# A graph network in two layers: edge maxima and the Wh sum moved forward on VectorE in even steps, divisions joined in odd steps, and a new order in the first five steps

## The chip, the cores and the metric

The kernel runs on one core of one Trainium2 chip. A core has a matrix engine (TensorE, PE in the profile; its weight loads, PEld, overlap the matmuls), VectorE (DVE), ScalarE (ACT), GpSimd (POOL) and SyncE (SP), each with a queue of its own that it works off in order. Data come from and go to DRAM through DMA, and here nearly all transfers are issued by SP. The metric is device time in microseconds; the number that counts is the median of the runs. One further execution was profiled, and its trace is what the text quotes.

## The reference

128 graphs of 128 nodes with 512 features each, and an integer adjacency matrix for each graph. Two layers, both with a residual and a layer norm:

```
# layer 0: attention with 8 heads of 64
q, k, v = x @ Wq + bq, x @ Wk + bk, x @ Wv + bv
attn    = softmax(where(adj > 0, q k^T / 8, -1e9))      # over the keys
x       = layernorm(x + relu(attn v @ Wo + bo))
# layer 1: graph attention with one head
Wh      = x @ W
e       = leaky(s_i + s_j),  s_i = Wh @ a1,  s_j = Wh @ a2   # leaky: slope 0.2
att     = softmax(where(adj > 0, e, -9e15), axis=1)     # over the senders
x       = layernorm(x + leaky(att @ Wh))
```

All is in fp32. Every product with a weight matrix is done by Strassen's scheme: seven products of half-size blocks in place of eight, with sums of blocks before and after.

## The kernel before, in words

The kernel is a software pipeline over graphs. Step t of the main loop (line 987) handles graph t in the first stage and older graphs in later ones. Graphs go in groups of four for Q, K and V (21 block products, `group_steps`), in pairs for the attention's output product with Wo (`LayerZero`) and for the product with W (`LayerOne`). `group()` takes the next block product of a group, `pair()` the next of a pair. An even step holds a pair's products with W, an odd step those with Wo. Everything stands in the order that the loop writes down; no scheduler moves it. So the text of the loop is the order in every engine's queue.

What one step contains, as far as the change touches it:

- Two softmaxes start in an even step, `first` for graph t and `sm` for t+1 (`Softmax`). `scores` are TensorE's matmuls into PSUM (tile lg). `add` adds the mask on VectorE (L534), `reduce` takes the negated row maxima (L543), `exp` is one ScalarE instruction for each head (L554), `reciprocals` two of VectorE (L564), `divide` one of ScalarE for each head (L568). `store` writes the weights to DRAM (pa_dram, L575), `fetch` reads them back in four pieces (paz, L581), `transpose` turns the 32x32 blocks on VectorE (L587), and `attend` is the product with v (p_oT, L600). `first` is divided in its even step, `sm` in the odd step after; both are attended at the end of the odd step.
- `Edge` is layer 1 for one graph, seven steps back. `sender` adds s_i to the mask on ScalarE (e, L798), `store_sender` and `fetch_sender` send it through DRAM, `turn_blocks` ends its transposition (L817), `add` adds s_j (L820), `maxima` is leaky and row maximum (L825, L827), `exp` L831, `divide` a reciprocal and a multiplication on VectorE (L835, L836), `product` is the matmul with Wh (p_h, L841). One step later the same object is called `fin`: `residual` (L851, L852), `stats`, `rstd` (GpSimd), `apply` (L665) and `store` (L865).
- Of the seven block products of a pair, p1, p6, p7 and p4 accumulate in one PSUM bank, p_y, one after the other. Between them ScalarE copies the bank out (pr_t, L459), and the next product may not start before that copy has read. `c11` is the first result block; for `LayerOne` it is VectorE's addition into wh (L772), whose last column is s_i, so `sender` needs it.
- For a group, the weight blocks of V are too large to stay and come through a ring of three tiles (wv_n, L408), loaded one by one.
- In steps divisible by four GpSimd forms the block sums of the next group's inputs (xS, L276 to L279).

The first steps fill the pipeline and have branches of their own (t below 3, t = 4), which also hold work that is done once, such as the sums w1_chores. From END on, a list written out by hand empties it.

Of the kernel before, what the change touches and what calls it, by code (L numbers as in the profile page):

```python
# [24 lines left out]
def kernel(  # L25
# [225 lines left out]
    def load_x(b):  # L251
        X[b] = spread(x[b])
# [734 lines left out]
    for t in range(-3, END):  # L987
        pair_steps = []
        if t % GROUP == 1 and on(t + 3):
            rest = group_steps  # L990
            group_steps, v_pieces, fetch_v = products((t + 3) // GROUP)
            group_steps = rest + group_steps
        if t % 2 == 1 and on(t - 3):
            pair_steps = zero[(t - 3) // 2] = LayerZero((t - 3) // 2)
            pair_steps = pair_steps.steps()
        if t % 2 == 0 and on(t - 6):
            pair_steps = LayerOne((t - 6) // 2).steps()

        def group(n=1):
            for _ in range(min(n, len(group_steps))):  # L1000
                group_steps.pop(0)()
            for _ in range(min((3 if t == -3 else 2 if t >= 0 else 1) * n, len(chores))):
                chores.pop(0)()

        def w1_chores(n):
            for op in [w1_sums.pop(0) for _ in range(n)]:
                op()

        def pair(n=1):
            for _ in range(min(n, len(pair_steps))):  # L1010
                pair_steps.pop(0)()

        if on(t + 2):
            load_mask(t + 2)
        if t == 0:
            load_blocks(Wo, columns(wo), nc.sync, spread_rows=False)
            late_chores = right_blocks(places(wo)) + load_bias()
            w1_loads, w1_sums, w1_blocks = load_w1()
        if t == 1:
            chores += late_chores  # L1020

        if t % 2 == 0:

            first, sm = none, none
            if on(t):
                first, sm = (Softmax(b, first_homes.get(b)) for b in (t, t + 1))
            first.scores()
            sm.scores()
        coming.turn_blocks()
        if t % 2 == 1 and on(t - 3):  # L1030
            zero[(t - 3) // 2].by()
            zero[(t - 3) // 2].bw()
        if later and t > 4:
            later.pop().go_back()
        if t % 2 == 1:
            sm.exp(6, 7)
        if t == 5:
            group(2)
        if t < 3 and t % 2 == 0:
            first.maxima()  # L1040
            sm.add(0)
            sm.add(1)
            group(2)
            if on(t - 2):
                load_residual(t - 2)
            if t == 0 and on(GROUP):
                sum_x(1)()
            first.exp(0, 1, 2, 3)
            group()
            first.reciprocals(0)  # L1050
            first.exp(4, 5, 6, 7)
            first.reciprocals(1)
            sm.reduce()
            first.divide(0, 1, 2, 3)
            if t == 2:
                held[1].transpose()
            group()
            first.divide(4, 5, 6, 7)
            mask_float(t + 2)
        elif t < 3:  # L1060
            group(2)
            if on(t - 2):
                load_residual(t - 2)
            group()
            sm.reciprocals(0)
            sm.reciprocals(1)
            if t == 1:
                group()
            sm.divide(0, 1, 2, 3)
            first.transpose()  # L1070
            group()
            sm.divide(4, 5, 6, 7)
            if t == 1:
                group()
            if on(t + 2):
                mask_float(t + 2)
        elif t == 4:

            layer = later.pop()
            first.maxima()  # L1080
            group()
            layer.apply(0)
            sm.add(0)
            sm.add(1)
            load_residual(2)
            if on(8):
                sum_x(2)()
            first.exp(0, 1)
            group()
            first.exp(2, 3, 4, 5)  # L1090
            sm.reduce()
            group()
            layer.store(1)
            layer.store(0)
            layer.fetch(1)
            layer.fetch(0)
            w1_chores(3)
            first.exp(6, 7)
            group()
            first.reciprocals(0)  # L1100
            first.reciprocals(1)
            first.divide(0, 1, 2, 3, 4, 5, 6, 7)
            mask_float(6)
        else:
            if t % 2 == 0:
                first.maxima()
            group()
            if t % 2 == 0:
                sm.add(0)
                sm.add(1)  # L1110
            if t == 3:
                w1_chores(3)
            if t == 5:
                turn_x1(4)
                x1_sums()
            edge = coming
            edge.add()
            fin.residual()
            if on(t - 2):
                load_residual(t - 2)  # L1120
            if t % 2 == 1:
                sm.reciprocals(0)
                sm.reciprocals(1)
            edge.maxima()
            fin.stats()
            fin.rstd()
            x1_sums()
            if t % GROUP == 0 and on(t + GROUP):
                sum_x(t // GROUP + 1)()
            if t % 2 == 0:  # L1130
                pair()
                first.exp(0, 1, 2, 3)
                edge.exp()
                pair()
                first.exp(4, 5)
                sm.reduce()
                group()
                first.reciprocals(0)
                pair()
                first.exp(6)  # L1140
                fin.apply()
                fin.store()
                first.exp(7)
                edge.divide()
                pair()
                first.reciprocals(1)
                first.divide(0, 1, 2, 3)
            else:
                pair()
                sm.divide(0, 1)  # L1150
                edge.exp()
                sm.divide(2)
                pair()
                sm.divide(3, 4, 5)
                first.transpose()
                group()
                pair()
                fin.apply()
                fin.store()
                sm.divide(6, 7)  # L1160
                sm.store()
                edge.divide()
                pair()
            coming = Edge(t - 6) if on(t - 6) and t + 1 < END else none
            coming.sender()
            coming.store_sender()
            if t in (3, 5):
                w1_chores(2 if t == 3 else 4)
            if t == 5:
                for op in w1_blocks:  # L1170
                    op()
            group()
            if t % 2 == 0:
                first.divide(4, 5)
            pair()
            if t % 2 == 0:
                first.divide(6, 7)
            if on(t + 2):
                mask_float(t + 2)
            group()  # L1180
        if t % 2 == 0:
            first.store()
        elif t < 3:
            sm.store()
        if 0 <= t < 3:
            for load in w1_loads[4 * t : 4 * t + 4]:
                load()
        if t % 2 == 1:
            sm.fetch()
        if t >= 6:  # L1190
            coming.fetch_sender()
        if t % 2 == 0:
            first.fetch()
        for b in x_turns(t):
            transpose_x(b)
        for b in x_turns(t + 1):
            load_x(b)
        if on(t + 2):
            mask(t + 2)
        if t % 2 == 0:  # L1200
            sm.exp(0, 1, 2)
        pair()
        if t % 2 == 1 and t != 1:
            sm.transpose()
        pair()
        if t % 2 == 0:
            sm.exp(3, 4, 5)
        if t % 2 == 0 and on(t - 6):
            turn_x1(t)
        if t not in (0, 4):  # L1210
            group(21 if t % GROUP == 0 else 1)
        fin = edge
        fin.product()
        fin.copy()
        if t == 1:
            held = first, sm
        elif t == 2 or t % 2 == 1:

            both = held if t == 2 else (first, sm)
            for softmax in both:  # L1220
                softmax.attend()
            for softmax in both:
                softmax.copy()
            both[1].sum(0, 1, 2, 3)
# [183 lines left out]
```

## Time and profile before

| what | value |
|---|---|
| median of 3 runs | 2463.04 us (2461.87 to 2465.6) |
| profiled execution, own time | 2459.1 us |
| span of the profile | 2457.2 us |
| mean granted TensorE clock | 0.997 |
| DMA, mean | 161 GB/s, 395 MB |

A line of the groups and waits names the engine, the source line and the tile it writes. "PE p_y L448 <- ACT pr_t L459: total, times, longest" tells for how long in all, how often and at most how long TensorE stood before a matmul of line 448 for ScalarE's line 459. A row of the timeline has the start, the time, the engine, the line and the operation, the tiles written and read, and, in brackets, the idle time before it with what ended it. A row of the table by stage has the stretch, its length, and for PE, PEld, DVE, ACT and POOL the busy time with the number of instructions, then the granted clock, the share of the DMA engines and GB/s. SPq is SP's queue; the time of its rows is that of issuing.

### The profile page before, as it was taken

Reading aid. Unit: us, or ns where it says so; the run is one execution under the profiler, and the core shown is the slowest. Engines: PE = TensorE matmul, PEld = TensorE weight load, DVE = VectorE, ACT = ScalarE, POOL = GpSimd, SP = SyncE. Lnnn points to the kernel's source line nnn. Section 1 sums busy time; section 2 is a strip of 40 time slices with the busy share of each in tenths; the row PEclk is TensorE's granted clock in tenths of the full one; section 3 lists DMA queues with packets and bytes.
Section 4 is the critical chain, followed back from the end, with each engine's and each line's share of the span. In section 5 each row is a group of like instructions: output and inputs, shape, how many; then the busy total and the mean of one; then the engine's idle time right before and its main releaser. Section 6 shows DMA issues by size and latency. Waiting matters only on the chain.

```text
span 2457.2 us, 44158 instructions
## 1 busy us (share of the span) xinstructions
PE 2355.6 (96%) x13362; PEld 1972.3 (80%) x13362; DVE 1836.2 (75%) x3718; ACT 1517.7 (62%) x5459; POOL 770.5 (31%) x1191
## 2 busy tenths in 40 slices
PE   8999999999999999999999999999999999999997
PEld 7788888888888888888888788878888888888775
DVE  5677777777777777777777777777777777777768
ACT  3656656666656566566565565665666656656675
POOL 1232332323333323333233332333332332323326
PEclk9999999999999999999999999999999999999999
DMA  7555555555555555555555555545554555545443
GB/s 203 163 157 158 164 161 171 158 155 170 160 154 165 159 162 162 165 166 156 158 160 164 161 163 154 169 153 164 167 159 151 170 165 162 163 154 169 145 159 115
DMA packets 435565, 395.31 MB, mean 161 GB/s; under 512 B 108280, under 2 KB 339328, under 8 KB 435328
## 3 DMA queue, kind: packets, MB, share of 16 engines
q1 hardware_dynamic: 435008, 392.23, 51.6%
q8 instruction: 107, 1.75, 0.3%
q14 instruction: 130, 1.06, 0.1%
q10 hardware_dynamic: 320, 0.26, 0.0%
HBM read 248.58 MB, written 143.72 MB: 160 GB/s over the span
## 4 chain that ended last, share of the span: by engine, by line
PE 45%; DVE 25%; DMA 11%; ACT 9%; SPq 4%; issue 4%; POOL 1%; DVEq 0%; POOLq 0%; ACTq 0%
PE st_y L367 14%; PE p_y L448 9%; PE st_w L367 7%; DMA pa_dram<-pa 5%; PE p_w L448 5%; DVE pa L534 4%; ACT pa L568 4%; PE st_x L367 3%; PE p_h L841 3%; SPq L581 3%; DMA ez<-e_dram 3%; DMA paz<-pa_dram 2%; DVE pa L587 2%; DVE nmax L543 2%; DVE z L665 2%
## 5 line engine op out<-in xcount | busy, mean ns | idle before, releaser
L650 POOL TENSOR_SCALAR ve<-mv 128x1 f32<-128x1 f32 x256 | 70.3, 275 | 1529.3 <-DVE mv L646 1521.9
L554 ACT ACTIVATE pa<-pa,nmax 128x128 f32<-128x128 f32 x1008 | 394.6, 397 | 9.8 <-DVE nmax L543 9.5
L568 ACT ACTIVATE pa<-pa,rs 128x128 f32<-128x128 f32 x1008 | 334.1, 396 | 33.9 <-DVE rs L564 33.9
L587 DVE STREAM_TRANSPOSE pa<-paz 128x1024 f32<-128x1024 f32 x126 | 156.9, 1245 | 89.0 <-DMA ez<-e_dram 58.3
L459 ACT COPY pr_t<-p_y 128x257 f32<-128x257 f32 (+1 forms) x375 | 138.1, 368 | 126.5 <-PE p_y L448 125.7
L348 ACT ACTIVATE st_t<-st_y,b_cols 128x256 f32<-128x256 f32 x192 | 80.1, 468 | 190.9 <-PE st_y L367 190.8
L554 ACT ACTIVATION_READ_ACCUMULATOR pa<-pa,nmax 128x1 f32 x1008 | 195.1, 194 | 0.0
L344 ACT COPY st_t<-st_y 128x512 f32<-128x512 f32 x192 | 111.0, 578 | 135.5 <-issue 78.9
L600 PEld LDWEIGHTS p_oT<-pa,v 128*64 128x64 f32 x2016 | 108.0, 136 | 89.0 <-DVE pa L587 41.7
L614 ACT ACTIVATE oT<-p_oT,b_cols 128x128 f32<-128x128 f32 x504 | 141.2, 375 | 59.7 <-PE p_oT L600 59.4
L448 PE MATMUL p_y<-w,x1T 128*128 128x257 f32 x496 | 134.3, 393 | 37.2 <-ACT pr_t L459 35.6
L600 PE MATMUL p_oT<-pa,v 128*64 128x128 f32 x2016 | 132.6, 278 | 33.5 <-DVE pa L587 32.9
L534 DVE TENSOR_TENSOR pa<-lg,mf 128x512 f32<-128x512 f32 x252 | 160.9, 679 | 0.2 <-PE lg L520 0.2
L543 DVE TENSOR_REDUCE nmax<-pa 128x8 f32<-128x1024 f32 x126 | 151.7, 1204 | 2.3
L652 POOL TENSOR_TENSOR rstd<-ve,mhalf 128x1 f32<-128x1 f32 x256 | 146.5, 572 | 21.3
L448 PEld LDWEIGHTS p_y<-w,x1T 128*128 128x128 f32 x496 | 89.4, 190 | 70.8 <-ACT pr_t L459 58.5
L448 PE MATMUL p_y<-wo,oT 128*128 128x256 f32 x504 | 130.5, 382 | 4.0 <-ACT p_y L469 4.0
L520 PE MATMUL lg<-kT,qT 64*128 64x128 f32 x2048 | 132.1, 279 | 0.0
L448 PE MATMUL p_y<-w,x1S 128*128 128x257 f32 x496 | 129.9, 384 | 0.4 <-ACT wk L459 0.2
L448 PE MATMUL p_y<-wo,oS 128*128 128x256 f32 x504 | 129.5, 379 | 0.6 <-ACT pr_t L459 0.5
L520 PEld LDWEIGHTS lg<-kT,qT 64*128 64x128 f32 x2048 | 119.4, 188 | 12.3 <-issue 11.9
L367 PE MATMUL st_y<-wv_n,xT 128*128 128x256 f32 x512 | 122.4, 382 | 2.6 <-ACT st_t L344 2.6
(201 smaller groups left out, 5902.6 us busy)
## 6 DMA issues: line engine op xcount, KB each, us to landing
pa_dram<-pa SPq DMA_DIRECT2D x126, 512.0 KB, 2.9
paz<-pa_dram SPq DMA_DIRECT2D x504, 128.0 KB, 2.8
wv_n<-wv SPq DMA_DIRECT2D x224, 256.0 KB, 2.9
x<-in_x_dram SPq DMA_DIRECT2D x128, 256.0 KB, 2.9
x_dram<-x SPq DMA_DIRECT2D x128, 256.0 KB, 2.1
xz<-x_dram SPq DMA_DIRECT2D x512, 64.0 KB, 2.0
xz<-in_x_dram SPq DMA_DIRECT2D x496, 64.0 KB, 2.1
out_dram<-z SPq DMA_DIRECT2D x120, 256.0 KB, 2.1
```

Source lines behind the costliest of these rows:

```text
L367: nc.tensor.matmul(p[:, m, :], lhs, rhs, start=start and m == 0 and kc == 0, stop=True, skip_group_check=True,)
L448: nc.tensor.matmul(p[:, :width], xs()[n][:, kc, :], w[:, PLACE[n], kc, :], start=start and kc == 0, stop=True, skip_group_check=True,)
L459: nc.scalar.copy(t[:, :width], p[:, :width])
L520: nc.tensor.matmul(self.lg[r][:, c, :], q[rows, c, cols], k[rows, c, cols], start=c == 0, stop=True, skip_group_check=True,)
L534: nc.vector.tensor_add(by_head[:, r * NC : (r + 1) * NC], self.lg[r].rearrange("p c (b k) -> p c b k", b=4), mf.unsqueeze(1).to_broadcast( ...
L543: nc.vector.tensor_reduce(self.nmax, by_head, AX.XY, ALU.max, negate=True)
L554: nc.scalar.activation(self.pa[:, :, h, :], self.pa[:, :, h, :], AF.Exp, bias=self.nmax[:, h : h + 1], accum_out=self.sums[:, h : h + 1],)
L568: nc.scalar.activation(self.pa[:, :, h, :], self.pa[:, :, h, :], AF.Copy, scale=self.rs[:, h : h + 1])
L587: nc.vector.transpose(self.paT.rearrange("p h (a i) -> p a h i", i=32), self.paz.rearrange("p a (h k) -> p a h k", k=32),)
L600: nc.tensor.matmul(self.oT[r * HD : (r + 1) * HD, c, :], v[:, h * HD : (h + 1) * HD], self.paT[:, r * NC + c, :], start=c == 0, stop=True, ...
L614: nc.scalar.activation(OT[pair][:, c, h * P : (h + 1) * P], self.oT[:, c, :], AF.Identity, bias=b_cols[:, 1, c : c + 1],)
L652: nc.gpsimd.tensor_tensor(self.r, ve, mhalf, ALU.pow)
```

## The change

The steps of the loop are reordered; no instruction is added or taken away.

- Even steps from 6 on: `edge.maxima` goes ahead of `sm.add` and `fin.residual`. The pair product with `c11` goes ahead of `edge.divide`, and `fin.apply` and `fin.store` go behind both and behind the second reciprocals. Heads 6 and 7 of `first` get their exponentials together.
- Odd steps from 3 on: heads 3 to 7 of `sm` are divided in one go and `sm.store` follows directly, ahead of `first.transpose` and of `fin.store`.
- First steps: at t = 0 a further group product stands between the exponentials of `first`, and `sm`'s exponentials of heads 3 to 7 are all in t = 1. At t = 4 the w1 sums go to the end of the branch and one load of x comes forward.

```diff
-        if t % 2 == 1:
+        if t % 2 == 1 and t != 1:
             sm.exp(6, 7)
...
             first.reciprocals(0)
-            first.exp(4, 5, 6, 7)
+            first.exp(4, 5)
+            if t == 0:
+                group()
+            first.exp(6, 7)
             first.reciprocals(1)
...
                 load_residual(t - 2)
+            sm.exp(3, 4, 5, 6, 7)
             group()
...
-            w1_chores(3)
+            for b in x_turns(5)[:1]:
+                load_x(b)
             first.exp(6, 7)
...
             mask_float(6)
+            w1_chores(3)
         else:
             if t % 2 == 0:
                 first.maxima()
             group()
-            if t % 2 == 0:
-                sm.add(0)
-                sm.add(1)
...
             edge.add()
-            fin.residual()
+            if t % 2 == 0:
+                edge.maxima()
+                sm.add(0)
+                sm.add(1)
+                fin.residual()
+            else:
+                fin.residual()
+                sm.reciprocals(0)
+                sm.reciprocals(1)
+                edge.maxima()
             if on(t - 2):
                 load_residual(t - 2)
-            if t % 2 == 1:
-                sm.reciprocals(0)
-                sm.reciprocals(1)
-            edge.maxima()
             fin.stats()
...
                 pair()
-                first.exp(6)
+                first.exp(6, 7)
+                pair()
+                edge.divide()
+                first.reciprocals(1)
                 fin.apply()
                 fin.store()
-                first.exp(7)
-                edge.divide()
-                pair()
-                first.reciprocals(1)
                 first.divide(0, 1, 2, 3)
...
-                sm.divide(3, 4, 5)
+                sm.divide(3, 4, 5, 6, 7)
+                sm.store()
                 first.transpose()
                 group()
                 pair()
                 fin.apply()
                 fin.store()
-                sm.divide(6, 7)
-                sm.store()
                 edge.divide()
                 pair()
...
-        for b in x_turns(t + 1):
+        for b in x_turns(t + 1)[t == 4 :]:
             load_x(b)
...
-        if t % 2 == 0:
+        if t % 2 == 0 and t != 0:
             sm.exp(3, 4, 5)
```

## The prediction

> **What bounds the kernel now.** I read the busy shares first, then who TensorE waits for, then the timeline of one cycle of four steps.
>
> ```profile
> PE 2355.6 (96%) x13362; PEld 1972.3 (80%) x13362; DVE 1836.2 (75%) x3718; ACT 1517.7 (62%) x5459; POOL 770.5 (31%) x1191
> ```
>
> TensorE is busy for all but 101.6 us of 2457.2, so a change of order can win at most about 100 us here. The list of TensorE's waits, from 240 to 2340 us:
>
> ```profile
> PE p_y L448 <- ACT pr_t L459: 34.5, 41, 1.2
> PE p_oT L600 <- DVE pa L587: 28.7, 31, 1.7
> ```
>
> Two waits are all there is in the loop. Where they sit shows in the table by stage, one row for each step (a multiple of 4, then t = 1, 2, 3 modulo 4 in other cycles):
>
> ```profile
> 1067.80:1092.50 24.70, 21.87 (x143) 18.10 (x142) 18.41 (x33) 15.54 (x58) 10.13 (x13) 1.00 0.50 154
> 1016.80:1032.40 15.60, 15.60 (x72) 13.34 (x72) 10.75 (x24) 8.06 (x27) 3.70 (x6) 1.00 0.59 177
> 1032.40:1052.30 19.90, 19.90 (x136) 16.71 (x135) 17.02 (x34) 15.11 (x59) 5.49 (x10) 1.00 0.47 155
> 1052.30:1067.80 15.50, 15.50 (x71) 13.28 (x70) 10.89 (x25) 8.26 (x26) 4.20 (x8) 1.00 0.52 163
> ```
>
> Odd steps run without a gap; the stretch around a step divisible by 4 has 2.8 us of idle TensorE. First wait, in the even step (timeline, us from the start):
>
> ```profile
> 1081.09 0.40 ACT L831 ACTIVATE att<-att,nmax 128x128 f32<-128x128 f32 x1 [1.40 <-DVE nmax L827]
> 1082.98 1.38 DVE L665 TENSOR_SCALAR z<-z,mv,rstd 128x512 f32<-128x512 f32 x1
> 1084.47 1.11 DVE L836 TENSOR_SCALAR att<-att,rt 128x128 f32<-128x128 f32 x1
> 1085.50 0.42 DVE L772 TENSOR_TENSOR wh<-p_x,pr_t 128x257 f32<-128x257 f32 x1
> 1085.95 0.40 ACT L798 ACTIVATE e<-mf,wh 128x128 f32<-128x128 bf16 x1 [0.90 <-DVE wh L772]
> 1086.84 0.35 ACT L459 COPY pr_t<-p_y 128x257 f32<-128x257 f32 x1
> 1087.24 1.14 PE L448 MATMUL p_y<-w,x1T 128*128 128x257 f32 x4 [1.17 <-ACT pr_t L459]
> ```
>
> The fourth product into p_y must wait for ScalarE's copy of that bank (pr_t). ScalarE is late because it stood 1.40 us for the edge maximum and 0.90 us for the sum for Wh; that sum stood on VectorE behind fin.apply and the edge division. Second wait, at the end of the odd step before:
>
> ```profile
> 1060.14 0.70 ACT L568 ACTIVATE pa<-pa,rs 128x128 f32<-128x128 f32 x2
> 1061.30 0.34 SPq L865 DMA_DIRECT2D out_dram<-z  x1
> 1061.74 0.38 SPq L575 DMA_DIRECT2D pa_dram<-pa  x1
> 1064.61 3.16 SPq L581 DMA_DIRECT2D paz<-pa_dram  x4
> 1070.22 1.25 DVE L587 STREAM_TRANSPOSE pa<-paz 128x1024 f32<-128x1024 f32 x1 [2.99 <-DMA ez<-e_dram]
> 1071.52 1.09 PE L600 MATMUL p_oT<-pa,v 128*64 128x128 f32 x16 [1.66 <-DVE pa L587]
> ```
>
> The odd softmax's weights go out to DRAM and come back (L575, L581) before VectorE turns them; the way out began only at 1061.74, behind the output store. (The wait is put down to ez; the transpose reads paz, so it is the four paz loads.)
>
> [...] pa's store stood 0.9 us behind a z store that waited for VectorE. [...] L665 takes 504 ns at least and 1387 at most, L836 285 and 1116; the long ones lie where GpSimd's sums for the next group run (t divisible by 4). L772, one of whose operands is in PSUM, stays at 0.42 us. [...] the mean clock is 0.66 in 51 to 56 us and 0.57 in 82 to 86 us.
>
> **The change, part by part.** No arithmetic is added or removed; it moves work.
>
> *(a) Even steps, edge maxima ahead (L825, L827).* They end at about 1078.6 instead of 1081.06, so the exponential follows the first four with no 1.40 us wait, and pr_t's second copy (the one TensorE needs at 1083.3) ends at 81.7. Behind the maxima stand sm.add and the residual, 0.57 us later; they free PSUM that only p_h needs, at 1092.5. The order up to sm.reduce is a permutation, so reduce and the first reciprocal end as before, at 1083.06.
>
> *(b) Even steps, sum for Wh ahead.* L772 runs at 1083.0 to 83.4 (its product p_x ended at 81.7). ScalarE: exponentials to 82.4, division of four heads from the reciprocal at 83.1 to 84.35, e without a wait to 84.7, heads 4 and 5 to 85.25, pr_t to 85.55. The fourth product is due at 1084.18 + 1.72 = 1085.90 (eight st matmuls start there, and eight take 1.72: 1089.09 to 1090.81 in the next pair): it stands no more, or 0.1. The order on TensorE and ScalarE is the same in even steps. Before, the product came at 1087.24 and the next, p_w, at 1088.22 (0.98 later instead of 0.87): 1.44 us lost. What gets late instead: fin.apply. L836 waits for GpSimd's first sum (to 1084.08) and ends at 84.2, fin.apply for the second (to 85.50) and ends at 85.75; then v's addition (0.65), then c22's Wh addition (0.43) at 86.85, which p_w, due at 86.75, reuses: 0.3 us of new wait. Net 1.44 - 0.1 - 0.3 = 1.0 us, in 29 steps (t = 8 to 120): 29 us. fin.store moves from 1084.39 to 85.8, and behind it in SP's queue e's store, the last wv_n load (1086.79, now 86.6), and pa's store. That wv_n landed after 2.65 us (1089.44); now at 89.3, for a product due at 89.7. Hidden, by 0.4 us.
>
> *(c) The other even steps* (t = 2 modulo 4): GpSimd is idle there, L665 takes 0.52. The loss is 1048.71 + 0.97 against 1046.84 + 1.72 + 0.87, 0.25 us; with the 0.15 us waits in a third of them I take 0.3. pr_t moves from 1048.29 to 47.4, so all goes: 30 x 0.3 = 9 us.
>
> *(d) Odd steps, divisions in one go, store ahead.* Heads 6 and 7 follow 3 to 5 directly and end at 1060.15 instead of 60.84; pa's store, no longer behind z's, starts at 60.2 instead of 61.74. No packet moved from 1059 to 1061.5. The store took 2.85 us to land; the loads are issued behind z, e and wv_n, at about 63.3 instead of 64.61: 1.3 us earlier. What pays: a group's copy (L344) and pr_t's second copy stand 0.69 us behind the two divisions, pr_t ends at 60.95, TensorE needs it at 61.77: hidden by 0.8. The k addition and fin.apply come 0.7 later on VectorE, hidden by its 0.96 us wait at 1063.24. TensorE's wait was 28.7 us in 31 cases; by the starts each costs 0.2 more (1071.52 against 1068.77 + 0.95), so 35 us. Their sizes run from 0.2 to 1.7, and 1.3 off each leaves a fifth: 28 us won.
>
> *(e) First five steps.* In 47 to 137 us TensorE stands 1.89, 0.36, 2.04, 0.73, 1.25, 1.68 and 3.09 us, 11.0 together, and two half-clock stretches cost about 1.5 each (eight matmuls took 3.16 instead of 1.89 and the next 2.45). A group step between the exponentials of t = 0 lets the copy that ends the 1.89 start at 49.2, when its product ends, instead of 50.46: 1.2 off, 0.7 stays. w1's six sums (4.3 us on VectorE, ahead of the reciprocals that ScalarE awaited for 3.42 us) go behind them: 1.25 and 1.68 go. The x load ahead of pa's store and the store itself help the 3.09. I take 10 of 14, with 3 and 14 as ends. The rest (single exponentials joined, the residual's load, whose neighbours in SP's queue stay) costs nothing: no queue is passed. The tail's plan is unchanged.
>
> Sum: 29 + 9 + 28 + 10 = 76 us. The profiled execution took 2459.1 us (span 2457.2), so 2383; the median of the runs is 3.9 above it, so 2463.0 - 76 = 2387.
>
> **Rivals.**
> *R1, SP's queue becomes the wait.* For: fin.store now waits 1.4 us longer ahead of e and wv_n; wv_n landed in up to 3.9 us elsewhere. Then TensorE stands 0.8 us for it (86.6 + 3.9 against 89.7): 29 x 0.8 = 23 lost, 2410. Against: 2.65 and 2.77 us in the cycles I read.
> *R2, the loads land no earlier.* For: the third paz load was held 1.83 us at its issue, and others were not (1.74 us for all four at 1027.6), so the transfers have their own queue. Then (d) brings nothing: 48 us, 2415.
> *R3, slower.* fin.apply does not get between GpSimd's four sums and waits for the last (1088.08): it ends at 88.4, c22's addition at 89.5, p_w at 90.05 instead of 88.22. That is 1.85 us more in each cycle of four, 29 x 1.85 = 54 us against the 47 of (c), (d), (e) then left: 2470. It decides once fin.apply ends after about 1088.1. Against: both tensor_scalars got in after one sum each.
> *R4, no change:* something not in these rows fills the gaps again, within 0.2% (5 us, about what a measurement of this kernel can tell).
>
> **Chances.** Forecast 0.62 (2368 to 2402), R1 0.16, R2 0.15, R3 0.05, R4 0.02. All waits gone would be 40 + 9 + 35 + 14, near 2368; the upper end reaches over R1 and R2 to 2421. Faster 0.93, same 0.02, slower 0.05.
>
> **What would show it.** In the list of waits, p_y on pr_t falls from 34.5 to under 5 us, p_oT on L587 from 28.7 to under 8, the edge exponential's wait for L827 goes from even steps. L665's longest stays near 1.4. A new line for p_w on wh, 5 to 10 us. Span from p_h to p_h near 22.0 in steps divisible by 4, 19.6 in the other even ones, odd ones unchanged. Wrong if a line wv_n or p_w stands at over 20 us, or if p_oT keeps its 28.

## The result and the profile after

The changed kernel takes 2420.73 us (median of 4 runs, 2415.22 to 2423.75), the kernel before, run beside it, 2464.32 us (2461.87 to 2466.06). The ratio is 0.9821, with a 95% interval of 0.9800 to 0.9842: 44 us were won where the prediction has 76. The time is 34 us above the forecast of 2387 and 0.3 us inside the upper end of the range (2421), which the prediction had drawn over its rivals R1 and R2. The profiled execution took 2422.03 us, its span is 2420.2 us, 37.0 less than that of before.

The busy shares of the page of after:

```profile
PE 2351.9 (97%) x13362; PEld 1978.1 (82%) x13362; DVE 1848.6 (76%) x3718; ACT 1512.3 (62%) x5459; POOL 770.6 (32%) x1191
```

TensorE still stands idle for 68.3 us. Its waits in the loop, from 240 to 2340 us (in total, times, longest):

```profile
PE p_oT L600 <- DVE pa L587: 18.5, 21, 1.8
PE st_w L367 <- DMA wv_n<-wv: 6.0, 10, 2.4
PE st_w L367 <- DVE x1T L246: 3.2, 14, 0.3
PE st_y L367 <- DMA wv_n<-wv: 2.7, 1, 2.7
```

The line p_y on pr_t (34.5 us before) is gone. The line p_oT has lost 10 of its 28.7 us, and a new wait for wv_n stands in two lines: st_w reads wv_n, and the line with x1T is taken for the same wait put down to another engine, since both go when wv_n comes earlier (below). The last line is a single wait in the tail, which now begins within this window.

The table by stage, for the same four steps as before (columns as there):

```profile
1007.80:1023.40 15.60, 15.60 (x72) 13.30 (x70) 10.98 (x25) 8.34 (x28) 3.99 (x8) 1.00 0.63 187
1023.40:1043.00 19.60, 19.60 (x136) 16.80 (x134) 16.88 (x34) 15.04 (x60) 5.18 (x9) 1.00 0.50 156
1042.60:1058.10 15.50, 15.50 (x71) 13.27 (x70) 10.79 (x25) 8.25 (x26) 4.09 (x8) 1.00 0.59 180
1058.10:1082.20 24.10, 22.04 (x143) 18.11 (x142) 18.68 (x33) 15.42 (x58) 10.24 (x13) 1.00 0.46 142
```

All idle time is again in the step divisible by four. Over the 28 cycles from p_h of step 11 on, the mean from p_h to p_h fell from 24.06 to 23.08 us in those steps and from 20.16 to 19.67 in the other even ones; odd steps stay at 15.5. That is 40 us in the loop. The part before it became 3.3 us longer (241.5 to 244.8), the tail did not change.

The even step of the last row, from the timeline (start, time, instruction, idle time before it):

```profile
1069.99 0.39 ACT L831 ACTIVATE att<-att,nmax 128x128 f32<-128x128 f32 x1
1073.49 0.40 DVE L772 TENSOR_TENSOR wh<-p_x,pr_t 128x257 f32<-128x257 f32 x1
1074.68 1.54 DVE L665 TENSOR_SCALAR z<-z,mv,rstd 128x512 f32<-128x512 f32 x1
1074.80 0.39 ACT L798 ACTIVATE e<-mf,wh 128x128 f32<-128x128 bf16 x1
1075.67 0.35 ACT L459 COPY pr_t<-p_y 128x257 f32<-128x257 f32 x1
1076.25 0.34 SPq L865 DMA_DIRECT2D out_dram<-z  x1
1076.27 1.03 PE L448 MATMUL p_y<-w,x1T 128*128 128x257 f32 x4
1076.68 0.38 SPq L806 DMA_DIRECT2D e_dram<-e  x1
1077.16 0.40 SPq L408 DMA_DIRECT2D wv_n<-wv  x1
```

Neither the edge exponential (L831) nor e waits any more, and the fourth product starts without a wait. On SP's queue the output store stood for fin.apply until 1076.25, and wv_n is issued third, at 1077.16; it landed at 1080.30, and the product that reads it (st_w) began at 1080.44, after TensorE had stood 0.30 us.

And the end of the odd step ahead of it:

```profile
1050.41 0.33 SPq L575 DMA_DIRECT2D pa_dram<-pa  x1
1052.28 0.34 SPq L865 DMA_DIRECT2D out_dram<-z  x1
1052.71 0.59 SPq L806 DMA_DIRECT2D e_dram<-e  x1
1053.39 0.41 SPq L408 DMA_DIRECT2D wv_n<-wv  x1
1053.89 1.81 SPq L581 DMA_DIRECT2D paz<-pa_dram  x4
1060.61 1.25 DVE L587 STREAM_TRANSPOSE pa<-paz 128x1024 f32<-128x1024 f32 x1 [3.10 <-DMA ez<-e_dram]
1061.91 0.33 PE L600 MATMUL p_oT<-pa,v 128*64 128x128 f32 x2 [1.76 <-DVE pa L587]
```

The product of this step stands 9.71 us ahead of before's. In that frame pa's store went from 61.74 to 60.12 (the prediction: 60.2) and the loads of paz from 64.61 to 63.60, but the last of them landed at 70.10, as before (70.09). TensorE waits 1.76 us here (1.66 before).

### The profile page after: what moved, and what is told of

Read it like the earlier page. It is cut to its first block, busy times and chain, and to the rows that moved or that the text cites. A ratio compares the mean times of both kernels' runs of the same rounds, so it can differ in the third digit from the quotient of the medians.

```text
span 2420.2 us, 44049 instructions
## 1 busy us (share of the span) xinstructions
PE 2351.9 (97%) x13362; PEld 1978.1 (82%) x13362; DVE 1848.6 (76%) x3718; ACT 1512.3 (62%) x5459; POOL 770.6 (32%) x1191
## 3 DMA queue, kind: packets, MB, share of 16 engines
q8 instruction: 107, 1.75, 0.3%
## 4 chain that ended last, share of the span: by engine, by line
PE 67%; DVE 12%; DMA 9%; SPq 4%; ACT 4%; issue 2%; POOL 1%; DVEq 0%; POOLq 0%; ACTq 0%
PE st_y L367 20%; PE p_y L448 13%; PE st_w L367 10%; PE p_w L448 6%; PE st_x L367 5%; PE lg L520 4%; PE p_x L448 4%; PE p_h L841 3%; PE p_oT L600 3%; DMA ez<-e_dram 3%; DMA paz<-pa_dram 2%; SPq L581 2%; DMA wv_n<-wv 2%; ACT pa L568 2%; DVE pa L587 2%
## 5 line engine op out<-in xcount | busy, mean ns | idle before, releaser
L568 ACT ACTIVATE pa<-pa,rs 128x128 f32<-128x128 f32 x1008 | 326.8, 392 | 72.4 <-DVE rs L564 72.2
L847 ACT COPY z<-p_h 128x512 f32<-128x512 f32 x120 | 70.4, 587 | 95.4 <-PE p_h L841 93.5
L448 PE MATMUL p_y<-w,x1T 128*128 128x257 f32 x496 | 128.3, 381 | 1.6 <-ACT wk L459 1.6
L367 PE MATMUL st_y<-xT,wk 128*128 128x256 f32 x512 | 125.9, 389 | 3.8 <-DVE qT L385 3.8
```

The source lines that it names most:

```text
L367: nc.tensor.matmul(p[:, m, :], lhs, rhs, start=start and m == 0 and kc == 0, stop=True, skip_group_check=True,)
L448: nc.tensor.matmul(p[:, :width], xs()[n][:, kc, :], w[:, PLACE[n], kc, :], start=start and kc == 0, stop=True, skip_group_check=True,)
L568: nc.scalar.activation(self.pa[:, :, h, :], self.pa[:, :, h, :], AF.Copy, scale=self.rs[:, h : h + 1])
```

## The experiments

T1 is my theory after these traces: even steps paid as forecast, less a new wait for wv_n, which stands on SP's queue behind the output store; in odd steps the loads of paz go out earlier but stand behind other transfers; and the new first steps lose time, because a transpose that waits for DRAM got in front of additions that TensorE needs. R is the rival named with each run. The table has the runs and what their traces show. Each ratio is to the kernel before on the same chip, whose medians were 2458.4 to 2464.3 us, so medians of different rows are not to be subtracted from 2464.3. "First p_h" is the start of the first product p_h (step 7), "by 4" and "other even" are the mean lengths of those steps in the loop:

| kernel | median us | ratio to before (95%) | first p_h | by 4 | other even |
|---|---|---|---|---|---|
| before | 2464.3 | 1 | 167.7 | 24.06 | 20.16 |
| changed | 2420.7 | 0.9821 (0.9800 to 0.9842) | 173.1 | 23.08 | 19.67 |
| even steps alone | 2428.7 | 0.9873 (0.9860 to 0.9887) | 170.4 | 23.28 | 19.76 |
| maxima alone | 2449.6 | 0.9964 (0.9951 to 0.9977) | 166.9 | 24.15 | 19.70 |
| sum for Wh alone | 2447.6 | 0.9947 (0.9928 to 0.9966) | 166.8 | 23.26 | 20.30 |
| odd steps alone | 2439.6 | 0.9918 (0.9904 to 0.9931) | 166.7 | 23.74 | 19.90 |
| first steps alone | 2467.3 | 1.0031 (1.0020 to 1.0043) | 172.5 | - | - |
| changed, without first steps | 2417.7 | 0.9826 (0.9813 to 0.9840) | 167.5 | - | - |
| changed, z behind paz | 2383.1 | 0.9691 (0.9670 to 0.9713) | 169.7 | 21.89 | 19.65 |
| changed, wv_n behind paz | 2389.9 | 0.9716 (0.9697 to 0.9736) | 172.2 | - | - |
| changed, z behind wv_n | 2401.4 | 0.9761 (0.9746 to 0.9776) | 171.9 | 22.43 | 19.65 |
| changed, transpose late | 2412.1 | 0.9811 (0.9795 to 0.9828) | 165.9 | - | - |
| changed, three moves | 2372.0 | 0.9646 (0.9629 to 0.9664) | 169.8 | 21.54 | 19.67 |
| changed, once more | 2416.1 | 0.9821 (0.9801 to 0.9840) | 171.7 | 22.90 | 19.66 |

### Even steps alone

```diff
-            if t % 2 == 0:
-                sm.add(0)
-                sm.add(1)
...
             edge.add()
-            fin.residual()
+            if t % 2 == 0:
+                edge.maxima()
+                sm.add(0)
+                sm.add(1)
+                fin.residual()
...
-                first.exp(6)
-                fin.apply()
-                fin.store()
-                first.exp(7)
-                edge.divide()
-                pair()
-                first.reciprocals(1)
+                first.exp(6, 7)
+                pair()
+                edge.divide()
+                first.reciprocals(1)
+                fin.apply()
+                fin.store()
```

> Only the even steps of the change (edge maxima ahead, sum for Wh ahead of fin.apply and the edge division); odd steps and first steps as in the kernel before. T1 (even steps paid as forecast, the joined divisions of odd steps paid only a third of their 28 us because the loads of paz land no earlier): 33 us won, about 2431 us; in the list of waits p_y on pr_t gone, p_oT on L587 still at 26 to 30 us, and a line st_w on wv_n of 6 to 14 us. R (odd steps paid 28 in full and the even steps only 15): about 2449 us. R' (the parts aid each other, so that each alone brings little): over 2450 us.

Measured: 30 us less than the kernel before on that chip. TensorE's waits in the loop (a fourth line is the single wait in the tail, 2.0 us):

```profile
PE p_oT L600 <- DVE pa L587: 28.3, 31, 1.7
PE st_w L367 <- DMA wv_n<-wv: 3.3, 8, 0.8
PE st_w L367 <- DVE x1T L246: 2.5, 11, 0.3
```

p_y on pr_t is gone, p_oT is as before, and wv_n appears, as T1 has it. Its two lines have 5.8 us here, 9.2 in the changed kernel, and 7.3 when that was run once more, so profiles of one kernel differ by as much.

### The two halves of the even part

The maxima alone (the part of the diff above from `sm.add` to `fin.residual`):

> The kernel before with only the order of the first VectorE work of even steps changed (edge maxima ahead of the mask additions and the residual). T1 (ScalarE's copy pr_t is late through two waits in a row, 1.40 us for the maxima and 0.90 us for the sum for Wh, and the second takes over what the first leaves): the exponential's 1.40 us wait is gone, the wait for wh grows to more than 2 us, p_y on pr_t falls from 34 us by less than 6; ratio 0.998 to 1. R (the 1.40 us wait is the main part): p_y on pr_t falls below 20 us, ratio below 0.994.

TensorE's waits in the loop with it:

```profile
PE p_y L448 <- ACT pr_t L459: 36.6, 28, 1.3
PE p_oT L600 <- DVE pa L587: 27.6, 30, 1.7
```

The sum for Wh alone (the rest):

> The kernel before with only the second half of even steps changed (sum for Wh ahead of fin.apply and the edge division), the maxima where they were. T1: ScalarE starts its exponentials 1.4 us later than with both and has 0.7 us of slack before the reciprocals, so half of the gain stays: p_y on pr_t at 15 to 25 us, ratio 0.992 to 0.995 (with both 0.987). R (the sum for Wh alone carries the even part): p_y on pr_t below 5 us, ratio near 0.987.

And with this one:

```profile
PE p_oT L600 <- DVE pa L587: 30.9, 34, 1.9
PE p_y L448 <- ACT pr_t L459: 6.7, 43, 0.2
PE st_w L367 <- DMA wv_n<-wv: 0.5, 1, 0.5
PE st_y L367 <- DMA wv_n<-wv: 0.3, 1, 0.3
```

Neither expectation was right on p_y's wait, for the first part or the second; the ratio of the second (0.9947) lies in T1's range. The two lists say why. I had taken both moves to share every even step. They work in different ones. With the maxima alone, p_y waits 28 times instead of 41: the other even steps are at their 19.7 us, and in the steps divisible by four nothing is won (24.15), since ScalarE's wait for the sum for Wh grows from 25.1 to 43.7 us in 28 cases. With the sum for Wh alone, the steps divisible by four go to 23.26, as far as with both, p_y's wait shrinking to 0.2 us each, and the other even steps stay at 20.30. So the maxima are worth about 13 us in the steps without GpSimd's sums for the next group, the sum about 22 us in those with them. The medians of the two add up to 20 us and not to 30; the runs with the sum alone spread over 12 us (2438.75 to 2450.37), and its trace is that of the quickest.

### Odd steps alone

```diff
-                sm.divide(3, 4, 5)
+                sm.divide(3, 4, 5, 6, 7)
+                sm.store()
                 first.transpose()
...
-                sm.divide(6, 7)
-                sm.store()
                 edge.divide()
```

> Only the odd steps of the change (heads 3 to 7 divided in one go, pa's store directly behind, ahead of the output store). T1: the store starts 1.3 us earlier and the loads of paz are issued about 1.1 us earlier, but land at most 0.5 us earlier; p_oT on L587 falls from 28.7 to about 18 us, p_y on pr_t stays at 34: about 2454 us. R (odd steps paid in full): p_oT under 8 us, about 2436 us.

TensorE's waits in the loop:

```profile
PE p_y L448 <- ACT pr_t L459: 31.8, 30, 1.2
PE p_oT L600 <- DVE pa L587: 19.1, 25, 1.7
```

p_oT is at 19.1 as T1 has it and not under 8. The time is 19 us less, where T1 had 10: besides 9 us in the steps divisible by four (24.06 to 23.74), 7 went in the other even ones (20.16 to 19.90). T1 had nothing there. With pa's store earlier, VectorE's transpose at their head starts 0.01 us after p_h on the mean instead of 0.31, the last copy pr_t at 15.88 instead of 16.17, and p_y waits less.

### The first steps

The first steps alone (the blocks of the diff for t = 0, 1 and 4), and the changed kernel without them:

> Only the first five steps of the change. T1 (the further group product at t = 0 brings VectorE's transpose, which waits for paz, in front of the sums for qT that TensorE needs): the mark of graph 4's last product comes 3 us later than before, a gap of about 3.7 us near 66 us with a stretch at half clock behind it; about 2467 us. R (the first steps paid their 10 us and the loss in the start comes from the other parts): about 2454 us.

> The changed kernel with the first five steps as in the kernel before. T1: the start is that of before (241.5 us to graph 4's last product) and the loop that of after (2068): about 2417 us, 3 less than after. R (the first steps paid 10 us): about 2431 us.

Alone they cost 8.5 us by the medians, more than T1's 3. Taken out of the changed kernel they make no difference that the intervals show (0.9826 against 0.9821). With the new first steps and nothing else moved there, the first p_h comes at 169.7 to 173.1 us in six profiles, with the old ones at 166.7 to 170.4 in six. Not all of that is loss: in the new order one group product more (eight matmuls, 1.7 us) stands ahead of the first p_h, and only from step 8 on are the two orders level. At the p_h of step 10 the means of the six are 3 us apart; for the changed kernel alone it is 229.3 and 227.9 us in its two profiles and 228.1 without the new first steps, which fits ratios that can't be told apart. The 10 us that the prediction booked are not there in any of them. The timeline of the changed kernel near 65 us:

```profile
63.92 1.25 DVE L587 STREAM_TRANSPOSE pa<-paz 128x1024 f32<-128x1024 f32 x1 [5.78 <-DMA paz<-pa_dram]
65.09 0.65 DVE L385 TENSOR_TENSOR qT<-st_x,st_t 128x512 f32<-128x512 f32 x1
65.67 0.67 DVE L385 TENSOR_TENSOR qT<-st_w,st_t 128x512 f32<-128x512 f32 x1
65.80 3.78 PE L367 MATMUL st_y<-xT,wk 128*128 128x256 f32 x8 [3.75 <-DVE qT L385]
```

The further group product at t = 0 did take 1.16 us off the gap near 50 us, as forecast. But TensorE then reaches its next group product earlier, and that needs a sum for qT which stands on VectorE behind a transpose that waits 5.78 us for paz. The table by stage shows the price behind the gap (columns as above):

```profile
65.80:72.60 6.80, 6.80 (x41) 5.49 (x41) 2.80 (x6) 0.88 (x2) 0.00 (x0) 0.57 0.98 253
```

The granted clock is 0.57 there: eight matmuls took 3.78 us instead of 1.89. To test the mechanism, the transpose goes behind the two sums:

```diff
             sm.divide(0, 1, 2, 3)
-            first.transpose()
             group()
...
             group(21 if t % GROUP == 0 else 1)
+        if t == 1:
+            first.transpose()
```

> The changed kernel, but at t = 1 VectorE's transpose of graph 0's weights, which waits for paz, stands behind the two sums for qT and the two x transposes instead of in front of them. T1: the gap of 3.75 us near 65.8 us is gone and with it the half clock behind it; the first p_h, at 173.1 in the changed kernel, comes 4 to 6 us earlier, near 168; ratio near 0.980. R (half clock and gap only move to the next product, because TensorE runs ahead of its data there anyway): first p_h stays within 1.5 us of 173.

The same stretch in the table by stage of that kernel:

```profile
65.80:72.60 6.80, 6.80 (x32) 6.00 (x33) 6.34 (x10) 3.64 (x15) 0.00 (x0) 1.00 0.67 206
```

The gap and the half clock are gone there, and the first p_h is at 165.9 instead of 173.1 us, in the same order of products. So the place of the transpose is the cause of that gap. A part came back later, though, as R expected of all of it: before a p_y product at 82.86 us TensorE now stands 3.55 us (1.11 in the changed kernel, 2.04 in the one before), at a mean clock of 0.83 from 80 to 100 us. The ratio, 0.9811, is not told from 0.9821, and in the other kernel with this move (below) the first p_h is at 169.8, so what the move is worth was not shown.

### What holds the loads of paz

The output store of odd steps behind the four loads:

```diff
                 fin.apply()
-                fin.store()
                 edge.divide()
...
         if t % 2 == 1:
             sm.fetch()
+            if t > 5:
+                fin.store()
```

> The changed kernel, but in odd steps the output store (z, 256 KB) is issued behind the four loads of paz instead of ahead of them. T1 (the loads of paz are issued 1.1 us earlier but stand behind the data of z, e and wv_n): they land 0.7 to 1 us earlier, p_oT on L587 falls from 18.5 us to about 8, about 9 us less than the changed kernel (ratio to the kernel before near 0.978). R (the instruction fetches that share the DMA engines, or the store's own landing, set it): p_oT stays at 15 to 20 us, ratio within 0.001 of 0.982.

The same cycle as above in its timeline:

```profile
1038.87 0.33 SPq L575 DMA_DIRECT2D pa_dram<-pa  x1
1039.90 0.33 SPq L806 DMA_DIRECT2D e_dram<-e  x1
1040.32 0.41 SPq L408 DMA_DIRECT2D wv_n<-wv  x1
1041.97 1.74 SPq L581 DMA_DIRECT2D paz<-pa_dram  x4
1043.82 0.38 SPq L865 DMA_DIRECT2D out_dram<-z  x1
1047.87 1.25 DVE L587 STREAM_TRANSPOSE pa<-paz 128x1024 f32<-128x1024 f32 x1 [1.90 <-DMA paz<-pa_dram]
1049.17 1.09 PE L600 MATMUL p_oT<-pa,v 128*64 128x128 f32 x16 [0.56 <-DVE pa L587]
```

And its four longest waits:

```profile
PE st_w L367 <- DMA wv_n<-wv: 5.5, 4, 2.5
PE st_y L367 <- DMA wv_n<-wv: 3.2, 1, 3.2
PE p_oT L600 <- DVE pa L587: 1.4, 3, 0.6
PE p_y L448 <- ACT wk L459: 0.8, 1, 0.8
```

p_oT falls to 1.4 us, and the kernel by 32 us (0.9821 to 0.9691 of before), where T1 said 9. The wv_n load of these steps behind paz, the store ahead, does nearly the same:

```diff
-                nc.sync.dma_start(ring[n], wv[n])
+                held_loads.append((ring[n], wv[n])) if hold else nc.sync.dma_start(ring[n], wv[n])
...
         if t % 2 == 1:
             sm.fetch()
+            hold.clear()
+            while held_loads:
+                nc.sync.dma_start(*held_loads.pop(0))
```

`hold` is set in steps t = 3 modulo 4 from 7 on.

> The changed kernel, but in steps t = 3 modulo 4 the wv_n load (256 KB) is issued behind the four loads of paz, the output store stays ahead. T1: as much data leaves paz's way as with the output store, so p_oT on L587 falls from 18.5 to about 8 us, unless wv_n itself, issued some 2 us later, becomes TensorE's wait (a line wv_n over 10 us would show it). R: p_oT stays at 15 to 20 us.

p_oT is at 1.6 us, the ratio 0.9716. So either transfer out of the way is enough, and R is out. Means over the 28 steps t = 3 modulo 4, in us from the first matmul of the attention product of the other graph (p_oT of `first`); the second one is due 0.95 later:

| | before | changed | z behind paz | wv_n behind paz |
|---|---|---|---|---|
| pa's store issued | -7.01 | -8.65 | -8.64 | -8.64 |
| first load of paz issued | -3.90 | -4.98 | -5.87 | -5.52 |
| last load of paz landed | 0.64 | 0.28 | -1.09 | -0.72 |
| TensorE's loss | 1.14 | 0.78 | 0.05 | 0.11 |

Of the 1.64 us by which the store went forward, 1.08 reached the issue of the loads and 0.36 their landing. With one 256 KB transfer fewer ahead, the loads are issued 0.5 to 0.9 us earlier (after the changed kernel's, SP's queue was still busy issuing wv_n: 53.39 + 0.41, then 53.89), and from first issue to last landing they take 4.8 us instead of 5.26. Both shares count: the second is 0.48 us with z behind paz and 0.46 with wv_n behind it.

Why 32 us and not 9: T1 left 8 us at p_oT, but a landing 1.37 us earlier clears it all but altogether (20 us by the starts of the matmuls), and so does one 1.00 us earlier, with wv_n behind paz. The other 12 us came from a side that I had not priced. VectorE stands at that transpose too, by its waits in the loop 59.5 us in the changed kernel and 18.3 here, and all its work of the next step queues behind it. In the steps divisible by four, fin.apply ends 16.99 us after p_h's first matmul in the changed kernel and 15.64 here, and wv_n, behind the output store that waits for it, lands at 21.11 and here at 19.87. TensorE was won only 0.73 us, so wv_n and the sum that p_w needs gained half a microsecond on it: the loss at wv_n falls by 6 us, from 17 to 11, and at p_w from 6.7 to 1.1.

### wv_n behind the output store

In even steps the store goes behind e's store and the last wv_n load:

```diff
                 fin.apply()
-                fin.store()
                 first.divide(0, 1, 2, 3)
...
             group()
             if t % 2 == 0:
+                if t > 4:
+                    fin.store()
                 first.divide(4, 5)
```

> The changed kernel, but in even steps the output store is issued behind e's store and the last wv_n load. T1 (the wv_n load is late because SP's queue stood at the output store for fin.apply): wv_n is issued 0.5 to 1 us earlier, the loss between the starts of st_y and st_w falls from 14 us to below 5, about 10 us less than the changed kernel (ratio near 0.978). R (the load is issued in time but the traffic makes it land late): loss stays above 10 us, ratio within 0.001 of 0.982.

SP's queue in the timeline:

```profile
1063.05 0.32 SPq L806 DMA_DIRECT2D e_dram<-e  x1
1063.46 0.38 SPq L408 DMA_DIRECT2D wv_n<-wv  x1
1064.10 0.34 SPq L865 DMA_DIRECT2D out_dram<-z  x1
```

These rows are from a step divisible by four. wv_n is issued 1.6 us earlier on the mean (16.35 after p_h instead of 17.95) and lands at 19.24 instead of 21.11. Both st_w lines are gone from the waits, p_oT stays (16.9), the ratio is 0.9761: 15 us less, T1 had 10. R is out.

### Three moves at once

The store behind paz in odd steps, behind wv_n in even ones, and the late transpose at t = 1; and the changed kernel itself beside it:

> The changed kernel with three moves at once: the output store behind the loads of paz in odd steps, behind the last wv_n load in even steps, and graph 0's transpose behind the sums for qT. T1: the 9 us that TensorE still loses for wv_n and p_w behind the first move go, and 4 to 6 us in the start: ratio near 0.963, all lines of TensorE's waits in the loop under 2 us. R (the second move brings nothing where VectorE is no longer late): ratio 0.967 to 0.970.

> The changed kernel itself, beside the others on the same chip: ratio 0.982, and, as the first steps differ from run to run by up to 3 us, 0.980 to 0.984.

The three longest of TensorE's waits in the loop, with the three moves:

```profile
PE st_y L367 <- DMA wv_n<-wv: 2.5, 1, 2.5
PE p_oT L600 <- DVE pa L587: 1.9, 3, 1.1
PE p_y L448 <- ACT wk L459: 1.6, 3, 0.8
```

2372.0 us, 44 us below the changed kernel on the same chip (2416.1) and 86 below the one before: twice the gain of the change, by the place of one store in odd and in even steps and of one transpose. Steps divisible by four take 21.54 us; the sum of the shortest distances between their products, an estimate of a step without a wait, is 21.38. The one wait for wv_n of 2.5 us is that in the tail. The first steps brought less than hoped (first p_h at 169.8). The ratio, 0.9646, is nearer to T1's 0.963 than to R's 0.967 to 0.970.

## Why the prediction was right and wrong

The losses of TensorE by the starts of its matmuls, over the 28 cycles, with the start of the program:

| place | won by forecast | won in the trace |
|---|---|---|
| p_y on pr_t, steps divisible by 4 | 42 less 3 | 40 |
| p_w on the Wh sum (new) | -9 | -7 |
| other even steps (c) | 9 | 14 |
| p_oT on the transpose (d) | 28 | 10 |
| wv_n (new; "hidden, by 0.4") | 0 | -17 |
| first five steps (e) | 10 | -3 |

**Right.** (a) and (b) in all that concerns the engines: the exponential's wait and p_y's are gone, p_w waits where it was said to, for c22's addition behind fin.apply and v's, and fin.apply gets between GpSimd's sums (1074.68 to 1076.22, beside the second of them), so R3 is out. (c) was sized at 9 and is 14, of which even steps alone give 11 (20.16 to 19.76) and the rest comes with (d). In (d) every engine's time came as worked out, the store within 0.1 us. Of the signs that the prediction names, p_y's wait and the steps of 19.6 us came; p_oT under 8 us (18.5) and steps divisible by four near 22.0 us (23.08) did not, and p_w on wh has no line of its own, though the starts show its loss.

**By luck.** That the time lies within the range is no merit of the sum. The forecast's own band, 2368 to 2402, was missed. R1 and R2, priced as alternatives, both came in part, and a start that lost time, which no rival has, came on top; together they end 0.3 us below an upper end that had been drawn for one of them. (The sum of all waits, 40 + 9 + 35 + 14, leads to 2365 where the prediction has 2368; nothing hangs on it.)

**Wrong, first: the step "1.3 off each" in (d).** It carried the earlier store to the landing of the loads one for one. They were issued 1.1 us earlier on the mean and landed 0.36 us earlier, because they now follow z, e and wv_n directly, where before these had gone out while SP waited for pa's landing. R2 named this outcome and gave a queue of the transfers' own as the reason, which was not shown; in the two runs with one transfer out of the way the last load landed 1.37 and 1.00 us earlier, so what stands ahead of the loads, on SP's queue and among the data, is the cause.

**Wrong, second: "Hidden, by 0.4" in (b).** wv_n was to go out 0.2 us earlier and to land 2.65 us after. Measured against TensorE's products, it is issued when it was before (14.25 us after the first matmul into lg, 14.24 before), chiefly because fin.apply, for which the store ahead of it waits, ends 0.2 us later than worked out (1076.22, in the prediction's frame 1085.93, where it has 85.75). And it landed 3.16 us after its issue on the mean (2.71 before). 0.4 us of cover is less than the two together, and on the mean it landed 0.4 us after the product was due. What made the flight longer was not shown. This is R1, at 17 us where it had 23.

**Wrong, third: (e).** The prediction took gaps of TensorE one by one and asked for each whether its cause goes. Those gaps did shrink: 1.89 us to 0.73, 1.25 to nothing, 1.68 to 0.66, 3.09 to 2.30. But new ones of 3.75, 1.74 and 0.75 us came between them, and another at p_oT of 1.64 us, so that TensorE stands 13.4 us from 45 to 175 us where it stood 11.0. What the prediction left out is what TensorE meets next when it is early. For the longest of the new gaps that is the place of the transpose on VectorE, which until then had cost nothing; the causes of the others were not tested.

**What also was missed:** that a late paz holds up VectorE (59.5 us at that transpose in the loop) and with it fin.apply, the output store and wv_n one step later. The prediction priced p_oT's wait at TensorE alone.

**Open:** the loads of paz land with some irregularity that has a period of three cycles. In the changed kernel, TensorE lost 1.02 us on the mean in the 9 steps in which a packet of the queue "q8 instruction" fell among the loads, 1.14 in 10 in which the loads were issued a microsecond later, and 0.15 in the 9 others. No run varies that packet alone, so how much of p_oT's wait is its doing was not shown. SP's rows show what delayed the loads in the ten: one issue ahead of them, nine times that of e's store, took 1.1 to 1.7 us instead of 0.4 to 0.6:

```profile
239.46 1.38 SPq L806 DMA_DIRECT2D e_dram<-e  x1
```

What lengthens it stays open. With z behind paz, it takes 0.33 us in each of the 28 steps; with wv_n behind paz it is still over 1.2 us in nine, and p_oT hardly waits.

## What to carry to other kernels

A transfer that is issued earlier need not land earlier by as much: here a store issued 1.64 us earlier brought the landing of the loads behind it forward by 0.36 us, and one 256 KB transfer fewer ahead of them by 1.00 to 1.37 us more. So list what stands ahead of a transfer on its queue at the new time, and put stores that nobody waits for behind loads that somebody does (32 us here, z behind paz). Price a late transfer on every engine that stands for it, not on the slowest one alone, because the work queued behind the waiting instruction is late as well: 12 of those 32 us came by way of VectorE, whose waits at the transpose fell from 59.5 to 18.3 us. And when a gap is closed, look for the next thing that the engine will now be early for: here one gap shrank by 1.16 us, and one of 3.75 us came behind it.

## What the runs showed of the hardware

- **A lower clock behind a gap, in some profiles only.** With the old first steps TensorE stands 1.9 to 2.0 us before a product near 51 us. In three profiles with that gap (before, even steps alone, maxima alone) the mean clock from 51.0 to 56.5 us was 0.69, in two (odd steps alone, sum alone) 1.00; in a sixth of that order, the changed kernel without the first steps, the gap was split into 0.71 and 1.04 us and the clock stayed 1.00. So a gap of this length went with a lower clock in three of five profiles; the 0.66 and the first half-clock stretch in the prediction are from one of the three. What decides it was not shown.
- **Packets of q8 among the data.** The page lists 107 packets of the queue "q8 instruction" with 1.75 MB, 16 KB each; the one in the odd step shown above ran on one engine for 958 ns, and from 1058.5 to 1060.1 us, while the last loads of paz were awaited, the DMA engines were busy at a share of 0.08. In the 9 steps with such a packet the four loads of paz landed within 2.7 us of each other, in the others within 1.9.
